# Reciprocal standard deviations computed on VectorE alone in a four-layer network on one core

## The chip, the cores and the metric

The kernel runs on one core of a Trainium2 chip. The metric is device time in microseconds (us) of one execution. The time before is the median of three runs. The profile is that of one more execution, with a time of its own.

## The reference

The input x has shape 2 x 64 x 64 x 128 and float32 values. Four layers follow each other, and each adds its result to x:

- layer 0: group norm over 32 groups of channels, then four-headed attention over 4096 tokens with a relative position bias, `softmax(q k / sqrt(32) + pos) v`
- layer 1: group norm, then a triangular multiplication: layer norm, gated projections, a product over one spatial axis, a second layer norm and a projection
- layer 2: layer norm, attention with `silu(scores * scores)` in place of a softmax, causal, plus a positional term; self and positional part are joined and pass a layer norm over 256 channels; then a mixture of 64 experts
- layer 3: layer norm, softmax attention; then a mixture of 8 experts

What the change touches is one expression, which every norm contains:

```python
v = jnp.var(x, axis=axis, keepdims=True)
return (x - m) / jnp.sqrt(v + eps)
```

The kernel takes means and variances on VectorE and needs `1/sqrt(var + eps)` for tiles of 128 partitions by n numbers, with n = 1, 4, 8, 24 or 32.

## The kernel before, in words

**The helper.** `rstd_parts` (L97 to L112) makes the reciprocal deviations of one tile. It adds eps on VectorE (L101, tile rs_v), takes the square root on ScalarE (L105, rs_s), the reciprocal on VectorE (L108, rs_r), and one Newton step on VectorE: q = -0.5 r r (L110), q = q v (L111), out = (q + 1.5) r (L112). It is a generator: where the caller asks for `apart`, it yields after L101; it always yields after the square root. Callers that schedule by hand run what stands between two yields as one piece. `rstd` (L92) runs all pieces at once.

**Who calls it.** 52 calls are executed:

- Layer 0 calls it through `tokens` (L438, n = 1) for each of two images: the first ahead of the attention loop, the second as pieces inside it. While the first runs, GpSimd builds the table `ka` (L301, 16 products of 32x1024) and VectorE waits on no one else. The result `gr` goes into the normalisation L447, that into the key projection L482, and from there by transfers into the first scores (L800).
- Layer 1 calls it through `group_scale` (L146, n = 1) twice, and through `ln_stats` (L158, n = 8) for 8 groups of the first norm (L1092) and 8 of the second (L1151, tiles named l1o). The compiler's scheduler orders these instructions; GpSimd multiplies at L1089, L1161 and L1183.
- Layer 2's attention calls it through `norm_stats` (L1325, n = 4, 4, 24 and 32) and through `join` (L1471, n = 4), once for each of 16 blocks of 512 queries.
- Layer 2's experts call `ln_stats` 8 times with n = 8 (L1726); layer 3's attention and experts call it for each image with n = 32 (L171 and around).

A fallback branch of layer 0 (around L904) holds calls too; it isn't executed.

**Layer 2's attention.** It is ordered by hand. One step k of a query block issues, in this order: eight score matmuls in two pairs (L1527; the PSUM tile `sc` has two buffers), the square of the first pair on ScalarE (L1541), the scaling of the second pair on VectorE (L1551) and its square on GpSimd (L1554), two silus on ScalarE of the two steps before (L1565), and the matmuls with the values of three steps before (L1579). After this a planner (`some`, L1302 to L1308) runs pieces of the work that is due: by the number of pieces left over the number of steps left it takes so many pieces from `chain` (keys, statistics, joins, outputs) and from `fill` (the positional matmuls L1428). The pieces of a join are: transposes and a copy (L1457); the statistics L1462 and L1463 and four products L1465; then rs_v with the square root; then reciprocal and Newton step. After it come the pieces of the output (L1480 to L1502). An instruction of a piece stands in its engine's queue behind what the step has issued, and ahead of all that the next step issues.

Of the kernel before, what the change touches and what calls it, by code (L numbers as in the profile page):

```python
# [8 lines left out]
F32 = mybir.dt.float32  # L9
AF = mybir.ActivationFunctionType  # L10
ALU = mybir.AluOpType
# [3 lines left out]
P = 128  # L15
# [23 lines left out]
class Net:  # L39
# [57 lines left out]
    def rstd_parts(self, out, var, eps, n, apart=False):  # L97

        nc = self.nc
        v = self.small.tile([P, n], F32, tag=f"rs_v{n}", name="rs_v", bufs=4 if n < 8 else 2)  # L100
        nc.vector.tensor_scalar(v, var, eps, None, ALU.add)  # L101
        if apart:
            yield
        s = self.small.tile([P, n], F32, tag=f"rs_s{n}", name="rs_s", bufs=4 if n < 8 else 2)
        nc.scalar.activation(s, v, AF.Sqrt)  # L105
        yield
        r = self.small.tile([P, n], F32, tag=f"rs_r{n}", name="rs_r", bufs=4 if n < 8 else 2)
        nc.vector.reciprocal(r, s)  # L108
        q = self.small.tile([P, n], F32, tag=f"rs_q{n}", name="rs_q", bufs=4 if n < 8 else 2)
        nc.vector.scalar_tensor_tensor(q, r, -0.5, r, ALU.mult, ALU.mult)  # L110
        nc.vector.tensor_tensor(q, q, v, ALU.mult)  # L111
        nc.vector.scalar_tensor_tensor(out, q, 1.5, r, ALU.add, ALU.mult)  # L112

    def group_stats(self, ps, b, xT=None):

# [2103 lines left out]
```

## Time and profile before

| What | Value |
|---|---|
| time before, median of three runs | 4488.38 us (4481.65 to 4494.05) |
| the profiled execution's own time | 4491.71 us |
| its span | 4489.8 us |
| PE (TensorE) busy | 4093.3 us, 91% |
| DVE (VectorE) busy | 2932.6 us, 65% |
| ACT (ScalarE) busy | 2488.6 us, 55% |
| POOL (GpSimd) busy | 912.0 us, 20% |
| activation table loads by L105 | 25, 1283 ns each |
| activation table loads in all | 52 |

The share of an engine is an average over four very different layers, so a share says little about one place. In timeline lines the columns are start and duration in us, the engine, the line, the operation, the tiles (out<-in), the sizes and the count; brackets give the idle time ahead of it and what ended it. An activation table load (ACT_TABLE_LOAD) is a ScalarE instruction which the compiler puts ahead of an activation of another family of functions; it is named by the line of that activation. PEld is TensorE's loading of weights.

### The profile page before, as it was taken

What the parts mean: (1) busy time and instruction counts of PE and PEld (TensorE: products, weight loads), DVE (VectorE), ACT (ScalarE), POOL (GpSimd) and SP (SyncE); (2) the same over time, 40 slices, a digit from 0 to 9 for tenths busy, and PEclk for the clock granted to TensorE, in tenths of its full rate; (3) what the DMA queues carried; (4) which work ended last, traced back from release to release, by engine and by line L of the source; (5) the groups of instructions that cost most, each with busy time, mean ns of one, the idle gap of its engine ahead of it and who ended that gap; (6) DMA issues with size and microseconds to landing.
All of it is one profiled execution on the core that took longest, in us unless ns stands there. A gap on an engine that the chain in (4) does not pass through costs nothing.

```text
span 4489.8 us, 66995 instructions
## 1 busy us (share of the span) xinstructions
PE 4093.3 (91%) x26440; PEld 1633.4 (36%) x26440; DVE 2932.6 (65%) x4641; ACT 2488.6 (55%) x3267; POOL 912.0 (20%) x667
## 2 busy tenths in 40 slices
PE   6999999999999948468999899998689999999979
PEld 3233333333333326322233223332364444444453
DVE  4888888998999979745566656656253333333358
ACT  3777777777777724235777688785123222322225
POOL 4110011020000030113455455552000000000015
PEclk7999999999999968678999999997889999999969
DMA  6453335454333300000000000002610000000001
GB/s 174 93 135 62 69 84 137 76 123 89 59 60 61 61 9 1 10 18 1 1 1 1 1 1 1 1 1 88 177 40 0 0 0 1 0 0 1 0 10 34
DMA packets 200764, 189.10 MB, mean 42 GB/s; under 512 B 83546, under 2 KB 137658, under 8 KB 200250
## 3 DMA queue, kind: packets, MB, share of 16 engines
q1 hardware_dynamic: 196986, 179.35, 18.1%
q10 hardware_dynamic: 3072, 4.34, 0.4%
q8 instruction: 210, 3.44, 0.3%
q0 software_dynamic: 384, 1.05, 0.1%
q14 instruction: 112, 0.92, 0.1%
HBM read 143.78 MB, written 45.09 MB: 42 GB/s over the span
## 4 chain that ended last, share of the span: by engine, by line
PE 47%; DVE 9%; ACT 4%; issue 1%; SPq 1%; DMA 1%; POOL 0%; DVEq 0%; ACTq 0%; POOLq 0%
PE oTl L1954 10%; PE scl L1937 10%; PE l2sc L1527 5%; PE l2pos L1428 5%; PE l2av L1579 5%; PE f3ex L2121 2%; ACT l2es L1565 2%; SPq L1682 1%; PE l2pu L1412 1%; DVE l2es L1551 1%; DVE l1t L1117 1%; ACT l2es L1541 1%; PE l2po L1486 1%; PE l3pq L1889 1%; PE prl L1976 1%
## 5 line engine op out<-in xcount | busy, mean ns | idle before, releaser
L813 DVE TENSOR_TENSOR l0acc<-l0acc,l0es 128x1024 f32<-128x1024 f32 x960 | 1230.6, 1282 | 133.1 <-ACT l0es L808 39.3
L808 ACT ACTIVATE l0es<-l0sc 128x1024 f32<-128x1024 f32 x1024 | 952.4, 1053 | 284.7 <-PE l0sc L800 267.8
L800 PE MATMUL l0sc<-l0mv,ka 64*64 64x512 f32 x8192 | 921.7, 596 | 21.1 <-DMA l0mv<-l0hd 16.3
L1962 DVE TENSOR_TENSOR accl<-accl,esl 128x1024 f32<-128x1024 f32 x240 | 294.0, 1225 | 520.1 <-ACT esl L1948 482.1
L1554 POOL TENSOR_TENSOR l2es<-l2es 128x1024 f32<-128x1024 f32 (+3 forms) x288 | 505.0, 1753 | 603.9 <-DVE l2es L1551 532.8
L1948 ACT ACTIVATE esl<-scl 128x1024 f32<-128x1024 f32 x240 | 245.5, 1023 | 547.0 <-PE scl L1937 547.0
L1565 ACT ACTIVATE l2es<-l2es 128x1024 f32<-128x1024 f32 (+3 forms) x576 | 533.3, 977 | 6.9 <-POOL l2es L1558 6.7
L800 PEld LDWEIGHTS l0sc<-l0mv,ka 64*64 64x64 f32 x8192 | 294.5, 132 | 640.9 <-ACT l0es L808 296.8
L1551 DVE TENSOR_SCALAR l2es<-l2sc 128x1024 f32<-128x1024 f32 (+3 forms) x272 | 306.4, 1126 | 297.2 <-PE l2sc L1527 294.5
L1937 PE MATMUL scl<-l3qT,l3kT 128*128 128x512 f32 x1024 | 482.4, 593 | 0.9 <-DVE l3v L1903 0.9
L831 PE MATMUL l0o<-l0es,l0v 128*32 128x512 f32 x4096 | 465.6, 595 | 0.0
L1954 PE MATMUL oTl<-esl,l3v 128*128 128x512 f32 x960 | 448.5, 592 | 0.0
L1541 ACT ACTIVATE l2es<-l2sc 128x1024 f32<-128x1024 f32 (+3 forms) x288 | 273.4, 949 | 261.3 <-PE l2sc L1527 258.2
L1527 PE MATMUL l2sc<-l2q,l2kT 32*128 32x512 f32 (+3 forms) x2304 | 340.5, 625 | 10.0 <-DVE l2es L1551 5.8
L1579 PE MATMUL l2av<-l2es,l2v 128*32 128x512 f32 (+3 forms) x2304 | 321.6, 579 | 8.8 <-ACT l2es L1565 8.7
L1428 PE MATMUL l2pos<-l2v,toe 128*32 128x512 f32 (+3 forms) x2304 | 299.5, 581 | 1.4 <-ACT l2v L1373 1.4
L745 POOL TENSOR_TENSOR l0os<-l0os,l0rr 128x512 f32<-128x512 f32 x32 | 63.2, 1975 | 1152.0 <-ACT l0rr L742 1091.3
L2133 POOL TENSOR_TENSOR f3part<-f3part 128x256 f32<-128x256 f32 x64 | 46.5, 726 | 1204.3 <-ACT f3part L2130 1204.3
L1937 PEld LDWEIGHTS scl<-l3qT,l3kT 128*128 128x128 f32 x1024 | 192.2, 190 | 231.1 <-issue 226.5
L1954 PEld LDWEIGHTS oTl<-esl,l3v 128*128 128x128 f32 x960 | 182.4, 190 | 229.6 <-issue 225.5
L831 PEld LDWEIGHTS l0o<-l0es,l0v 128*32 128x32 f32 x4096 | 121.4, 109 | 304.1 <-issue 299.5
L1527 PEld LDWEIGHTS l2sc<-l2q,l2kT 32*128 32x128 f32 x2304 | 100.9, 189 | 255.0 <-ACT l2es L1565 91.7
(468 smaller groups left out, 3915.6 us busy)
## 6 DMA issues: line engine op xcount, KB each, us to landing
l0mv<-l0hd SPq DMA_DIRECT2D x254, 128.0 KB
l0mv<-l0qd SPq DMA_DIRECT2D x124, 256.0 KB
f2w<-in_L_ffn_weight_dram SPq DMA_DIRECT2D x16, 1024.0 KB
f2w<-in_L_ffn_weight_dram SPq DMA_DIRECT2D x64, 256.0 KB
l0mv<-l0wd SPq DMA_DIRECT2D x126, 128.0 KB
l0sh<-l0eh SPq DMA_DIRECT2D x60, 144.0 KB
l0tw<-l0sw SPq DMA_DIRECT2D x64, 128.0 KB
l0wd<-l0rw SPq DMA_DIRECT2D x16, 512.0 KB
```

Of the source, the lines that this page charges most:

```text
L800: nc.tensor.matmul(sc[64 * c : 64 * c + 64, h, :], lhsT=ka[rows, k0 : k0 + 64], rhs=mv[rows, NX - 1 - yb, :], start=True, stop=True,)
L808: nc.scalar.activation(es[yb, s], sc, AF.Exp)
L813: nc.vector.tensor_tensor(cur.acc, cur.acc, es[yb, s], ALU.add)
L831: nc.tensor.matmul(cur.o[lo : lo + HD, :], lhsT=v[:, 2 * (xb * NX + yb) + s, HD * h : HD * (h + 1)], rhs=es[yb, s][:, h, :], start=(xb == ...
L1428: nc.tensor.matmul(pos[c : c + 32, j0:, :], lhsT=toe[:, d * P + c : d * P + c + 32], rhs=v[:, n0 + j0 - d : n0 + 4 - d, :], start=(d == n0 ...
L1527: nc.tensor.matmul(sc[:, h2, off:], lhsT=kT[hs, cols], rhs=q[hs, off:], start=True, stop=True,)
L1551: nc.vector.tensor_scalar(es[:, :, lo:], sc[:, :, lo:], root, None, ALU.mult)
L1554: nc.gpsimd.tensor_tensor(part, part, part, ALU.mult)
L1565: nc.scalar.activation(e[:, :, off:], e[:, :, off:], AF.Silu)
L1579: nc.tensor.matmul(avs[i][hs, off:], lhsT=vs[b][:, k, hs], rhs=es[h // 2][:, h % 2, off:], start=(k == 0), stop=last,)
L1937: nc.tensor.matmul(sc[:, i, :], lhsT=kT[:, k * P : (k + 1) * P], rhs=qs, start=True, stop=True,)
L1954: nc.tensor.matmul(oT, lhsT=v[:, k, :], rhs=es[:, i, :], start=(k == 0), stop=(k == NC - 1),)
```

## The change

The square root on ScalarE and the reciprocal go. A first value of the reciprocal root is made from the bits of v, read as an integer: bits times -0.5 plus 0x5F3759DF, read as a float again. Three Newton steps follow in place of one. The fixed yield stands after the first Newton step now; the yield of `apart` stays where it was.

```diff
         nc.vector.tensor_scalar(v, var, eps, None, ALU.add)
         if apart:
             yield
-        s = self.small.tile([P, n], F32, tag=f"rs_s{n}", name="rs_s", bufs=4 if n < 8 else 2)
-        nc.scalar.activation(s, v, AF.Sqrt)
-        yield
         r = self.small.tile([P, n], F32, tag=f"rs_r{n}", name="rs_r", bufs=4 if n < 8 else 2)
-        nc.vector.reciprocal(r, s)
+        nc.vector.tensor_scalar(
+            r.bitcast(mybir.dt.int32),
+            v.bitcast(mybir.dt.int32),
+            -0.5,
+            float(0x5F3759DF),
+            ALU.mult,
+            ALU.add,
+        )
         q = self.small.tile([P, n], F32, tag=f"rs_q{n}", name="rs_q", bufs=4 if n < 8 else 2)
-        nc.vector.scalar_tensor_tensor(q, r, -0.5, r, ALU.mult, ALU.mult)
-        nc.vector.tensor_tensor(q, q, v, ALU.mult)
-        nc.vector.scalar_tensor_tensor(out, q, 1.5, r, ALU.add, ALU.mult)
+        for i in range(3):
+            nc.vector.scalar_tensor_tensor(q, r, -0.5, r, ALU.mult, ALU.mult)
+            nc.vector.tensor_tensor(q, q, v, ALU.mult)
+            nc.vector.scalar_tensor_tensor(out if i == 2 else r, q, 1.5, r, ALU.add, ALU.mult)
+            if i == 0:
+                yield
```

In the built order of instructions, PE, POOL and SP keep theirs. ACT loses 52 square roots, and its table loads fall from 52 to 6. DVE has six instructions more in each call, 312 in all that are executed: eleven instead of five. In layer 1 and in layer 2's experts they stand between the statistics of the next group; in the parts ordered by hand they stand together, as the pieces say.

## The prediction

> **What bounds the kernel now.** I read the page first, then all instructions of the square root's line, then timelines where it stands. The page says that TensorE is the wide bound, with VectorE second:
>
> ```profile
> PE 4093.3 (91%) x26440; PEld 1633.4 (36%) x26440; DVE 2932.6 (65%) x4641; ACT 2488.6 (55%) x3267; POOL 912.0 (20%) x667
> ```
>
> The line of the square root, with shortest, median and longest in ns:
>
> ```profile
> L105 ACT ACTIVATE rs_s<-rs_v x52: 203/208/229, 18.7 to 4306.0; 128x8 f32<-128x8 f32 x24, 128x4 f32<-128x4 f32 x18, 128x32 f32<-128x32 f32 x5, 128x1 f32<-128x1 f32 x4
> L105 ACT ACT_TABLE_LOAD  x25: 1283/1283/1283, 12.5 to 4304.7; - x25
> ```
>
> The reader sees what can be won at most: 52 roots of 0.208 us, and 46 of 52 loads (25 here, the others where the previous function is loaded back) of 1.283 us, 69.8 us of ScalarE, an engine 45% idle. What counts is the place. The first call is in layer 0, before any attention:
>
> ```profile
> 10.20 19.86 POOL L301 TENSOR_TENSOR ka<-l0rev 32x1024 f32<-32x1024 f32 x10
> ...
> 18.54 0.16 DVE L101 TENSOR_SCALAR rs_v<-gpv 128x1 f32<-128x1 f32 x1 [0.74 <-PE gpv L436]
> ...
> 18.97 0.16 DVE L108 RECIPROCAL rs_r<-rs_s 128x1 f32<-128x1 f32 x1 [0.27 <-ACT rs_s L105]
> 19.16 0.61 DVE L110 SCALAR_TENSOR_TENSOR rs_q<-rs_r 128x1 f32<-128x1 f32 x1
> ...
> 19.81 1.85 DVE L111 TENSOR_TENSOR rs_q<-rs_q,rs_v 128x1 f32<-128x1 f32 x1
> ...
> 21.69 1.85 DVE L112 SCALAR_TENSOR_TENSOR gr<-rs_q,rs_r 128x1 f32<-128x1 f32 x1
> ```
>
> One number per partition takes 0.16 us with one SBUF operand and 1.85 us with two, while GpSimd multiplies (1.99 us each, 16 until 34.7): every such step waits for one GpSimd product. Elsewhere L110 takes 0.17 at the median and 1.87 at most. Laid over GpSimd's products, 29 of 52 L110 lie free (mean 0.16 us) and 23 overlap (mean 1.23), while the reciprocal is at 0.20 either way.
>
> The second place is a join of layer 2's attention, 16 in all. Its chain of waits, then its timeline:
>
> ```profile
> 2171.69 1.28 ACT L105
> 2172.97 0.01 issue
> 2172.98 0.20 ACT rs_s L105
> 2173.18 0.91 ACT l2es L1541
> 2174.10 0.02 issue
> 2174.11 1.28 ACT L1565
> ```
>
> ```profile
> 2174.61 1.89 POOL L1554 TENSOR_TENSOR l2es<-l2es 128x1024 f32<-128x1024 f32 x1 [0.63 <-DVE rs_r L108]
> 2174.65 1.87 DVE L110 SCALAR_TENSOR_TENSOR rs_q<-rs_r 128x4 f32<-128x4 f32 x1
> ...
> 2176.84 1.22 DVE L1551 TENSOR_SCALAR l2es<-l2sc 128x1024 f32<-128x1024 f32 x1
> ...
> 2177.47 1.05 PE L1579 MATMUL l2av<-l2es,l2v 128*32 128x512 f32 x4 [0.37 <-ACT l2es L1565]
> ```
>
> Both loads lie on the chain. But in the same step VectorE's L110 waits for GpSimd's square, and L1551, which frees a score buffer, stands behind it. The third place is layer 1, from the windows:
>
> ```profile
> core 0: us, PE busy (x) PEld busy (x) DVE busy (x) ACT busy (x) POOL busy (x), PEclk, DMA share, GB/s
> 1640.00:1720.00 80.00, 34.10 (x128) 23.91 (x127) 64.42 (x219) 17.96 (x35) 24.71 (x15) 0.59 0.00 1
> ...
> 1935.00:3095.00 1160.00, 1073.57 (x7801) 342.76 (x7800) 680.44 (x1129) 854.10 (x966) 568.35 (x368) 0.96 0.00 1
> ```
>
> In layer 1's norm VectorE is busy 64 of 80 us and TensorE 34: what VectorE gets more of is paid there, and ScalarE's loads cost nothing. In layer 2's attention TensorE leads with 1074 of 1160.
>
> **Part by part.** A call loses a root (0.21) and a reciprocal (0.16 to 0.20), and gets the seed and six two-operand steps more. No row shows a product on integers; L101 has the same shape (0.16), and I take it, so the seed pays for the reciprocal. Were its conversion as dear as another whole instruction, it would be 52 x 0.16 = 8 us at most; nothing suggests that it costs less than L101. Dependent small steps start 0.20 us apart (1653.53, .73, .93 in layer 1); six are 1.2 us where nothing else fills the gaps, and 0.08 to 0.17 each between other instructions.
>
> *Start of layer 0.* Three waits for a product become nine: six more of 1.88 us (start to start) are 11.3. Without ScalarE's round trip (18.73 to 18.97) the seed starts at once, -0.2. VectorE is then done at 34.8, just as GpSimd ends, and the first normalisation L447 takes 0.8 us, as it does alone, not 2.4: -1.6. Sum +9.5 (7 to 11.5). Projections, transfers and the first score at 87.3 follow in series, TensorE standing idle for 14.5 us before that score, so nothing hides it.
>
> *Second call in layer 0.* Inside a loop where TensorE is busy 1483 of 1500 us; at its two loads (429.96 and 434.30) it idles 0.77. I take -0.5.
>
> *Layer 1.* First norm: 8 groups x 0.8 (between 0.5 filled and 1.2 dependent; more with GpSimd's 24.7 of 80 us, which stalled L110 for 1.65 in one group) and two group norms x 0.9: +8 (4 to 13). Second norm: VectorE sets a period of some 8.7 us, 8 x 0.7 = +5.5 (3 to 11). Nothing is gained: ScalarE is busy 18 of 80.
>
> *Layer 2's statistics.* n = 24 at the start, TensorE waiting for them: 1.2 less the round trip 0.4, +0.8. n = 32 in the loop: two loads go, taken like a join's below, -1.5.
>
> *Joins.* Gone: 2.77 us of ScalarE in two neighbouring steps. These took 4.34 and 5.06 us against 2.93 to 3.06 of others; the first was late because VectorE was still at the join's L1465. TensorE's values waited from 2176.04 to 2177.47: 1.4 us, which I take as the gain. Added: the seed and three steps in one piece, six in the next. The first piece now meets the square of 2172.09 (before, only L101 stood there): VectorE reaches L1551 1.0 to 1.4 us later. The second piece, about 2.8 us with one wait, lets the next L1551 start 1.7 us later than before. VectorE has 1.1 us of slack in a step, and TensorE needs the buffer: 0.4 + 0.75 lost. Net -0.25 each, **-4** for 16. If the delays hide, -1.4 x 16 = -22; if both are paid in full, +1.25 x 16 = +20.
>
> A rule of the Trainium skill speaks against the change here (SBUF — State Buffer, "Who interferes with whom"): a VectorE instruction with two SBUF inputs and a GpSimd instruction that reads SBUF exclude each other for a whole instruction, in order of issue. Read alone, it lets each of six added steps wait for a square of 1.89: 11.3 us a join, +181 in all. The row says how often: one L110 of 1.87 and then L111 and L112 of 0.16 each, because GpSimd does one square a step, which starts only after L1551. So a piece meets one, and I take one more wait a join. On the other side the Trainium skill (ScalarE: Activation LUTs, "What ACT_TABLE_LOAD costs") puts a switch at 1.28 us plus a drain of 1.38, which would make 46 of them 122 us; here a load ends at 2175.39 and silu starts at 2175.41, so it is 59 us.
>
> *Layer 2's experts*, 8 calls, VectorE busy 80% of a period, six steps of 0.08 to 0.2 each: 0.4 a call, +3 (0 to 6). *Layer 3's norms*: 1.2 less the longer part of the round trips, +0.7; *its experts' second norm*, where the reciprocal waited 2.61 us for ScalarE at 4306.23 and TensorE idled 1.19: -1.2.
>
> Sum: 9.5 - 0.5 + 8 + 5.5 + 0.8 - 1.5 - 4 + 3 + 0.7 - 1.2 = **+20.3**. The profiled execution would take 4491.7 + 20.3 = 4512.0 (span 4489.8 and 1.9 around it); it lay 3.3 above the median of the runs, so the forecast is 4488.4 + 20.3 = **4508.7**.
>
> **The rivals.**
>
> *The other side, faster: loads on ScalarE's chain.* Near the end of the image ScalarE itself runs from piece to piece in the chain, and a join's pieces show 1.28 + 0.20 + 1.28 = 2.76 us in it. If that is what a join is worth and VectorE's delays hide, 16 x 2.76 = -44 in place of -4, so 4508.7 - 40 = 4468.5. It wins over the rest from a price of 1.5 us a join (24.3 / 16), and shows as faster from 2.4. Against it: part of these loads lay where TensorE still had work, and VectorE is the next in line in just these steps.
>
> *Within 0.3%: layer 1 hides it.* The gaps of the scheduled parts take the added steps, and layer 2's experts too: 13.5 + 3 becomes 5: 4508.7 - 11.5 = 4497. For it: interleaved instructions start 0.08 us apart. Against it: the steps depend on each other.
>
> *Slower still: joins bound by VectorE.* Both delays paid, +20 in place of -4: 4533.
>
> *That the change doesn't do what it says* is excluded: six loads are left in the built order.
>
> **The numbers.** Some 0.3% (13.5 us) is what a measurement of this kernel can tell, so "same" is 4475 to 4502. The forecast has a chance of 0.5, joins bound by VectorE 0.2, hidden in layer 1 0.2, faster 0.1. The forecast's own range, 4496 to 4522, reaches a little below 4502, so slower gets 0.67, same 0.25, faster 0.08. The range goes from 4486, where joins gain half of what the rival says, to 4533.
>
> **What would show it.** L110 to L112 of the first call at 1.85 us nine times, L447's first at 0.8 and the first score near 97; layer 1 some 13 us longer; no load in joins, the values no longer late, but L1551 late behind rs_q and score matmuls waiting for it. I am wrong if joins get over 1 us shorter, or if GpSimd's products no longer hold up VectorE at the start.

## The result and the profile after

The changed kernel takes 4512.97 us (median of five runs, 4511.44 to 4518.77), against 4488.0 before (now the median of five runs): a ratio of 1.0057, 95% interval 1.0046 to 1.0069. That is 25.0 us slower; the forecast was 4508.7, 20.3 slower.

The profiled execution is the slowest of the five; its span is 4516.7 us, 26.9 above that of before. First the busy line of its page:

```profile
PE 4094.2 (91%) x26440; PEld 1644.2 (36%) x26440; DVE 3000.4 (66%) x4953; ACT 2422.7 (54%) x3169; POOL 910.6 (20%) x667
```

ScalarE lost 66 us of the 70 counted beforehand. VectorE has 312 instructions and 68 us more. At the 0.16 us of a free small instruction 312 would be 50, and the 52 seeds stand for the 52 reciprocals: by this estimate some 18 us more of VectorE's busy time is waiting. The timeline of the first call in layer 0 (VectorE alone) shows the waits (rows left out are marked "...", here and below):

```profile
18.74 0.15 DVE L105 TENSOR_SCALAR rs_r<-rs_v 128x1 int32<-128x1 int32 x1
18.93 0.86 DVE L115 SCALAR_TENSOR_TENSOR rs_q<-rs_r 128x1 f32<-128x1 f32 x1
19.82 1.85 DVE L116 TENSOR_TENSOR rs_q<-rs_q,rs_v 128x1 f32<-128x1 f32 x1
...
25.46 0.16 DVE L116 TENSOR_TENSOR rs_q<-rs_q,rs_v 128x1 f32<-128x1 f32 x1
25.66 1.77 DVE L117 SCALAR_TENSOR_TENSOR rs_r<-rs_q,rs_r 128x1 f32<-128x1 f32 x1
...
33.12 0.81 DVE L454 TENSOR_SCALAR l0mv<-l0xT,gm,gr 128x1024 f32<-128x1024 f32 x1
```

Seven of nine two-operand steps take 1.77 to 1.85 us, one 0.86, and one slips through at 0.16. The normalisation starts at 33.12 in place of 23.57, and is quick (0.81), GpSimd being nearly done. The join that the prediction looked at, 22 us later, with GpSimd's squares (POOL):

```profile
2194.35 1.90 POOL L1561 TENSOR_TENSOR l2es<-l2es 128x1024 f32<-128x1024 f32 x1 [2.93 <-DVE rs_v L101]
2194.38 1.89 DVE L105 TENSOR_SCALAR rs_r<-rs_v 128x4 int32<-128x4 int32 x1
...
2196.70 0.16 DVE L117 SCALAR_TENSOR_TENSOR rs_r<-rs_q,rs_r 128x4 f32<-128x4 f32 x1
2196.78 1.22 DVE L1558 TENSOR_SCALAR l2es<-l2sc 128x1024 f32<-128x1024 f32 x1
...
2198.05 0.30 PEld L1534 LDWEIGHTS l2sc<-l2q,l2kT 32*128 32x128 f32 x4 [0.52 <-DVE l2es L1558]
2198.08 1.89 POOL L1561 TENSOR_TENSOR l2es<-l2es 128x1024 f32<-128x1024 f32 x1 [1.84 <-DVE rs_q L115]
2198.11 1.89 DVE L116 TENSOR_TENSOR rs_q<-rs_q,rs_v 128x4 f32<-128x4 f32 x1
```

Each piece waits once for GpSimd, 1.89 us. In the first piece it is the seed that waits, an instruction with one tensor operand. The chain of waits at this join no longer holds ScalarE, but VectorE's L1558 and then TensorE:

```profile
2193.14 1.14 DVE l2es L1558
...
2194.32 1.13 PE l2sc L1534 x4
...
2197.30 1.88 PE l2sc L1534 x8
```

A step of before that nothing holds up has this row in its chain:

```profile
2180.10 1.07 PE l2sc L1527 x8
```

That is the price: eight score matmuls take 1.88 us instead of 1.07, because the second pair waits for L1558 (the PEld row at 2198.05), which stood behind the seed.

TensorE has the same 26440 matmuls in the same order in all kernels of this study (in candidates a and b two in layer 2's experts change places). So a stage can be measured between the same two matmuls in each trace. The table is worked out in that way, in us. Its first column runs from TensorE's first matmul; layer 1 is two stretches, of before about 1607 to 1722 and 1810 to 1893; a join is measured from the start of the third step behind its transposes to that of the sixth:

| Kernel traced | start, to the first projection | layer 1, both norms | join, three steps, mean of 15 |
|---|---|---|---|
| before | 20.97 | 199.2 | 12.25 |
| after | 28.97 | 217.1 | 12.36 |
| root in joins | 28.94 | 215.0 | 12.24 |
| scalar operands at the start | 17.28 | 215.5 | 12.36 |
| two Newton steps | 24.76 | 208.9 | 12.11 |
| root but in some places | 21.01 | 199.4 | 12.39 |
| joins in PSUM | 28.93 | 217.2 | 11.29 |
| layer 1 in PSUM | 28.74 | 192.8 | 12.36 |
| candidate a | 17.18 | 193.1 | 11.29 |
| candidate b | 17.48 | 194.9 | 11.39 |
| candidate c | 17.25 | 194.5 | 12.19 |
| two-step candidate | 17.25 | 193.3 | 11.25 |

Of the 26.9 us between the spans, 8.0 lie at the start, 18.0 in layer 1, and 1.7 in joins (15 x 0.11). The experts of layer 3 give back 1.4. What is left, some +0.6 net, is a sum of larger differences of both signs. The largest is a stage of layer 2's attention, from 2000 to 2120, which took 7.3 us less after than before. Other kernels show 115 and 120 us there with the root in the joins, and 113 to 120 without. The stage between the same matmuls, by windows of before and after, with TensorE's granted clock in the column PEclk:

```profile
core 0: us, PE busy (x), PEclk, DMA share, GB/s
2000.00:2120.00 120.00, 103.37 (x614) 0.87 0.00 1
```

```profile
2030.00:2142.00 112.00, 95.46 (x610) 0.94 0.00 1
```

The clock is 0.87 in one and 0.94 in the other, TensorE is busy for 168 and 156 ns a matmul, and no call of the helper stands there. Layer 0's loop took 4.7 more, 1518 before and 1523 after, and scatters up to 1528 over the traces. Its first stretch, from 110 to 420, lies ahead of the second call, and its code is that of before: it takes 310 us before, 312 after, and up to 318 in other traces.

### The profile page after: what moved, and what is told of

Its sections match the earlier page's. It is cut to its first block, busy times and chain, and to the rows that moved or that the text cites. A ratio compares the mean times of both kernels' runs of the same rounds, so it can differ in the third digit from the quotient of the medians.

```text
span 4516.7 us, 67206 instructions
## 1 busy us (share of the span) xinstructions
PE 4094.2 (91%) x26440; PEld 1644.2 (36%) x26440; DVE 3000.4 (66%) x4953; ACT 2422.7 (54%) x3169; POOL 910.6 (20%) x667
## 4 chain that ended last, share of the span: by engine, by line
PE 47%; DVE 12%; issue 2%; ACT 1%; DMA 1%; SPq 1%; POOL 0%; DVEq 0%; ACTq 0%; POOLq 0%
PE oTl L1961 10%; PE scl L1944 10%; PE l2sc L1534 6%; PE l2pos L1435 5%; PE l2av L1586 4%; PE f3ex L2128 2%; DVE l2es L1558 2%; PE l2pu L1419 1%; SPq L1689 1%; DVE l1t L1124 1%; PE l2po L1493 1%; DMA f2w<-in_L_ffn_weight_dram 1%; PE l3pq L1896 1%; PE f3pl L2062 1%; PE prl L1983 1%
## 5 line engine op out<-in xcount | busy, mean ns | idle before, releaser
L1558 DVE TENSOR_SCALAR l2es<-l2sc 128x1024 f32<-128x1024 f32 (+3 forms) x272 | 306.5, 1127 | 272.5 <-PE l2sc L1534 272.2
L1534 PE MATMUL l2sc<-l2q,l2kT 32*128 32x512 f32 (+3 forms) x2304 | 353.8, 615 | 14.4 <-DVE l2es L1558 6.2
L1586 PE MATMUL l2av<-l2es,l2v 128*32 128x512 f32 (+3 forms) x2304 | 306.6, 573 | 0.8 <-ACT l2es L1572 0.8
```

Source lines behind the costliest of these rows:

```text
L1534: nc.tensor.matmul(sc[:, h2, off:], lhsT=kT[hs, cols], rhs=q[hs, off:], start=True, stop=True,)
L1558: nc.vector.tensor_scalar(es[:, :, lo:], sc[:, :, lo:], root, None, ALU.mult)
L1586: nc.tensor.matmul(avs[i][hs, off:], lhsT=vs[b][:, k, hs], rhs=es[h // 2][:, h % 2, off:], start=(k == 0), stop=last,)
```

## The experiments

Every ratio is to the kernel before, run beside the experiment; the interval is the 95% one. The forecasts start from the changed kernel's 4513. The diffs show the decisive lines alone.

**Root kept in the joins.** The changed kernel, with a parameter:

```diff
-                yield from self.rstd_parts(rs[i], mv[:, :, 1], 1e-3, 4)
+                yield from self.rstd_parts(rs[i], mv[:, :, 1], 1e-3, 4, how="sqrt")
```

> The changed kernel, with the square root on ScalarE and one Newton step kept in the 16 joins alone. Theory: a join is nearly a wash, because the seed and the added steps put a second wait for GpSimd's square ahead of L1551's scaling and so give back what the two table loads cost; the two traces laid over each other put a join at -0.3 us. Undone in the joins: 4513 + 16 x 0.3 = 4518 us (4513 to 4521). Rival: the loads are worth what the chain shows, 2.76 us each: 4513 + 44 = 4557. Other rival: joins are bound by VectorE and cost 1.25 each now: 4493.

Measured: 4519.72 (4512.36 to 4525.85), ratio 1.0073 (1.0060 to 1.0086). Both rivals, 4557 and 4493, are out. The size is read from the table: 12.24 against 12.36, so undoing it in the joins gains 0.12 us each, 2 in all. The median stands above that of the changed kernel all the same, and their intervals overlap: that it came out near the 4518 of the expectation is luck. The -0.3 of the expectation was the join that I had looked at (13.04 to 12.72, as did six others by 0.3 to 0.5); six got 0.1 to 0.2 longer, and those at 2296 and 2706 got 1.6 longer. Beside these two, TensorE multiplies the values of short diagonal steps (128x384, 128x256 and 128x128 in place of 128x512), so it has less to do and the late L1558 can show in full; that this is the reason was not tested.

**Scalar operands at the start.** Only in the first call:

```diff
-            nc.vector.scalar_tensor_tensor(q, r, -0.5, r, ALU.mult, ALU.mult)
-            nc.vector.tensor_tensor(q, q, v, ALU.mult)
-            nc.vector.scalar_tensor_tensor(out if i == 2 else r, q, 1.5, r, ALU.add, ALU.mult)
+            nc.vector.tensor_scalar(q, r, r, -0.5, ALU.mult, ALU.mult)
+            nc.vector.tensor_scalar(q, q, v, 1.5, ALU.mult, ALU.add)
+            nc.vector.tensor_scalar(out if i == 2 else r, r, q, None, ALU.mult)
```

> The changed kernel, but in the first call of layer 0 (n = 1) each Newton step is written with one tensor operand and its other factors as per-partition scalars; as many instructions, in the same order. Theory: the start loses 7.7 us because two-operand instructions wait for GpSimd's products; with one operand each takes 0.16 us, the result is there near 20.9 in place of 33.1, the first normalisation is slow again (2.4 in place of 0.8), and the first projection comes some 10.5 us earlier: 4513 - 10.5 = 4502.5. Rival: the number of dependent steps costs it, whatever their operands are: 4513. Should the scalar operands wait for GpSimd too, it is 4513 as well, and the trace shows durations of 1.85.

Measured: 4505.51 (4497.09 to 4516.16), ratio 1.0044 (1.0031 to 1.0057). VectorE's timeline of the same nine steps, the first and last, and GpSimd's products beside them:

```profile
18.92 0.21 DVE L148 TENSOR_SCALAR rs_q<-rs_r 128x1 f32<-128x1 f32 x1
...
20.91 0.21 DVE L150 TENSOR_SCALAR gr<-rs_r,rs_q 128x1 f32<-128x1 f32 x1
21.16 3.35 DVE L495 TENSOR_SCALAR l0mv<-l0xT,gm,gr 128x1024 f32<-128x1024 f32 x2
```

```profile
17.83 8.46 POOL L347 TENSOR_TENSOR ka<-l0rev 32x1024 f32<-32x1024 f32 x4
```

As many instructions, as dependent as before, and GpSimd is multiplying beside them: none waits. The first projection comes 11.7 us earlier than after, and 3.7 earlier than before; the medians lie 7.5 apart, and their intervals just meet, so the stage shows it more clearly than the whole. It was the second tensor operand, not the count.

**Two Newton steps.** In every call:

```diff
-        for i in range(3):
+        for i in range(2):
```

> The changed kernel with two Newton steps in place of three in every call, three VectorE instructions fewer a call. Theory: the loss is paid by the added steps: at the start 3 waits of 1.88 go and the normalisation gets slower by 1.6 (-4), layer 1 gets back half of its 18 us (-9), layer 2's experts -1.5, a join -0.3 (-5): 4513 - 19 = 4494. Rival: the loss belongs to the call as such, to the seed's integer form and to the root that no longer overlaps: 4511.

Measured: 4493.57 (4488.15 to 4512.36), ratio 1.0014 (1.0007 to 1.0020), as the theory of the steps has it. Against the changed kernel, the start is 4.2 us shorter, layer 1 8.2 and a join 0.25. This run takes away instructions and waits together; the runs with PSUM below part them.

**The change only where it should gain.** Seed and three steps in joins, layer 0's second call, the second image's statistics and layer 3; elsewhere `how="sqrt"`.

> The seed and three steps only in joins, in layer 0's second call, in the statistics of layer 2's second image and in layer 3; the square root of before at the start, in layer 1, in layer 2's first statistics and in its experts. Theory: only places that gain are left: joins -5, second call -1.2, statistics -1.5, layer 3 -2.3, so 4488 - 10 = 4478 (4472 to 4484). Rival, that the differences seen in layer 2's attention are TensorE's clock and not the change: 4488.

Measured: 4488.10 (4485.67 to 4497.82), ratio 1.0000 (0.9992 to 1.0008). The theory of this run falls. The 5 us put down to the joins were the -0.3 of one join, taken 16 times: the table has the joins at 12.39 in the mean, 0.14 worse than before and so +2 in all, while layer 3's experts give back 1.4. The number of the rival came true; its reason, TensorE's clock, holds for the stage from 2000 to 2120, which takes 120 us here as before.

**Joins without waits.** The step is regrouped so that each instruction has one operand in SBUF and one in PSUM, the memory that TensorE writes its products to; v and e lie in columns of the join's own bank, read out by then:

```diff
-            nc.vector.scalar_tensor_tensor(q, r, -0.5, r, ALU.mult, ALU.mult)
-            nc.vector.tensor_tensor(q, q, v, ALU.mult)
-            nc.vector.scalar_tensor_tensor(out if i == 2 else r, q, 1.5, r, ALU.add, ALU.mult)
+            nc.vector.tensor_tensor(e, v, r, ALU.mult)
+            nc.vector.scalar_tensor_tensor(e, e, -0.5, r, ALU.mult, ALU.mult)
+            nc.vector.scalar_tensor_tensor(out if i == 2 else r, e, 1.5, r, ALU.add, ALU.mult)
```

> The changed kernel, but in the joins the Newton steps are regrouped as e = v r, e = -0.5 e r, r = (e + 1.5) r with v and e in PSUM, in columns of a bank that the join has already used: as many instructions, each with one SBUF operand. Theory: a join gains nothing because two waits for GpSimd's squares (1.9 us each) stand ahead of L1551's scaling. Without them the values no longer wait for the table loads and nothing is late in their place: some 1.3 us a join, 4513 - 20 = 4493 (4486 to 4500). Rival: the plain length of eleven small instructions makes L1551 late, waits or not: 4511.

Measured: 4499.03 (4493.02 to 4505.34), ratio 1.0023 (1.0014 to 1.0032). VectorE's timeline at the same join, and GpSimd's square beside it:

```profile
2204.17 0.16 DVE L127 TENSOR_SCALAR rs_r<-l2st 128x4 int32<-128x4 int32 x1
2204.36 0.17 DVE L140 TENSOR_TENSOR l2st<-l2st,rs_r 128x4 f32<-128x4 f32 x1
...
2205.36 1.23 DVE L1600 TENSOR_SCALAR l2es<-l2sc 128x1024 f32<-128x1024 f32 x1 [0.43 <-PE l2sc L1576]
```

```profile
2204.14 1.89 POOL L1603 TENSOR_TENSOR l2es<-l2es 128x1024 f32<-128x1024 f32 x1 [2.93 <-DVE l2st L106]
```

The square runs from 2204.14 to 2206.03, and seed and steps pass beside it at 0.16 to 0.17 each, and none of the helper's 176 rows in the 16 joins takes more than 0.18; the scaling now waits for TensorE (0.43), not TensorE for it. A join takes 11.29, so 1.07 less than after (16 us in 15 joins) and 0.96 less than before. The plain length of eleven small instructions is nearly hidden.

**Layer 1 without waits.** The same regrouping in layer 1's 16 layer norms, with a PSUM tile of their own.

> The changed kernel, with the regrouped steps (v and e in PSUM) in layer 1's 16 layer norms alone. Theory: of the 18 us that layer 1 got longer, six plain instructions a call explain about 12 (16 x 6 x 0.12), and waits for GpSimd the rest; in PSUM the waits of the steps that were there before go too, as far as they don't move to the next instruction: 4513 - 12 = 4501. Rival: only the number of instructions counts, since VectorE does them one after the other and GpSimd's work must be done anyway: 4513.

Measured: 4495.46 (4481.12 to 4505.77), ratio 1.0014 (1.0006 to 1.0023). Layer 1's norms take 192.8 us: 24.3 less than after, twice what I expected, and 6.4 less than before. A norm in the trace of after shows the waits, with GpSimd's product above the seed:

```profile
1660.56 2.35 POOL L1096 TENSOR_TENSOR l1y<-l1y,l1gb 128x1024 f32<-128x1024 f32 x1 [5.76 <-DVE mv_l L163]
1660.75 2.19 DVE L105 TENSOR_SCALAR rs_r<-rs_v 128x8 int32<-128x8 int32 x1
...
1662.97 1.18 DVE L115 SCALAR_TENSOR_TENSOR rs_q<-rs_r 128x8 f32<-128x8 f32 x1
1664.19 1.18 DVE L116 TENSOR_TENSOR rs_q<-rs_q,rs_v 128x8 f32<-128x8 f32 x1
```

Three waits in a row, the seed's the longest. The corresponding norm with v and e in PSUM:

```profile
1654.39 2.34 POOL L1144 TENSOR_TENSOR l1y<-l1y,l1gb 128x1024 f32<-128x1024 f32 x1 [4.45 <-DVE mv_l L204]
1654.58 0.17 DVE L127 TENSOR_SCALAR rs_r<-rs_l 128x8 int32<-128x8 int32 x1
1654.78 0.17 DVE L140 TENSOR_TENSOR rs_l<-rs_l,rs_r 128x8 f32<-128x8 f32 x1
```

Counted over the helper's rows of these 16 calls, what exceeds 0.175 us a row is 28.7 us before, 35.4 after and 0.0 here. So most of what this run takes away is waiting that was there before the change; the change added 6.7 us of waiting and, in 96 more rows, some 14 us of plain instructions.

**Candidates.** The first kernel, candidate a, puts together what the experiments showed to gain: scalar operands in layer 0 and the group norms, the root with one regrouped step in layer 1's layer norms, seed and three regrouped steps in the joins, the root of before in layer 2's first statistics and experts. Candidate b has the seed in layer 1 too; candidate c the root with one regrouped step in the joins; the last is a with two steps in joins, second statistics and layer 3.

```diff
-                yield from self.rstd_parts(rs[i], mv[:, :, 1], 1e-3, 4)
+                at = [pt[:, 0, 4 * k : 4 * k + 4] for k in range(2)]
+                yield from self.rstd_parts(rs[i], mv[:, :, 1], 1e-3, 4, at=at)
```

> A candidate to beat both: scalar-operand steps in layer 0 and in the group norms; ScalarE's root and one regrouped step with v and e in PSUM in layer 1's layer norms; seed and three regrouped steps in PSUM in the joins; the kernel of before in layer 2's first statistics and experts. Theory of the waits: start -4, layer 1 -8, joins -18, layer 3 -2 against before: 4488 - 32 = 4456 (4450 to 4470). Rival, that only the number of instructions counts: start and layer 3 alone, 4483.

> The same candidate, but with the seed and three regrouped steps in PSUM in layer 1 too: six VectorE instructions more a call than the other candidate, and no root. Theory: the plain price of the six, 0.1 each between other instructions, 16 x 0.6 = 10 us above it: 4466. Rival, that the waits were all that cost: equal to it.

> The first candidate with ScalarE's root in the joins too, and one regrouped step with v and e in PSUM: the two table loads are back in each join, six VectorE instructions a join are gone, and nothing waits for GpSimd in either. It prices the loads by themselves. Theory: a join's loads hold up the values by 1.4 us, as the trace of before showed at one join, so 4460 + 16 x 1.4 - 16 x 0.2 = 4479. Rival: without the waits ScalarE's loads hide beside the rest: 4460.

> The first candidate with two Newton steps in place of three in the joins, in the second image's statistics and in layer 3. Theory: without waits for GpSimd, three instructions more of 0.17 to 0.2 in a step with 1.1 us of slack cost a join 0.2 at most: 4460 - 3 = 4457, not to be told from the candidate. Rival: VectorE bounds the joins' steps, and each instruction counts in full: 4460 - 16 x 0.5 = 4452.

| Candidate | median us | lowest to highest | ratio to before (95%) |
|---|---|---|---|
| a | 4459.98 | 4449.55 to 4474.29 | 0.9932 (0.9917 to 0.9947) |
| b | 4464.37 | 4454.78 to 4469.85 | 0.9940 (0.9926 to 0.9955) |
| c | 4470.78 | 4468.32 to 4472.89 | 0.9960 (0.9947 to 0.9974) |
| two steps | 4457.22 | 4450.50 to 4465.89 | 0.9931 (0.9917 to 0.9945) |

All four beat both kernels. Candidate a stands 4 us off its forecast; the table's stages say where it gains: start 3.8, layer 1 6.1, joins 14.4 (15 x 0.96). Candidate b costs 1.8 us in layer 1's norms, not 10: six instructions more a call that wait for nothing are nearly paid for by the root's round trip that goes, and by the gaps between others. The plain instructions of the change are cheap there because nothing waits any more. Candidate c prices the loads where nothing waits for GpSimd: a join of 12.19 against 11.29, 0.90 us net of six small instructions, less than the 1.4 of the expectation and not zero. At the join that the 1.4 was read from it is 1.37 (13.01 against 11.64). Two steps in place of three are not told from a by the runs (0.04 a join).

## Why the prediction was right, point by point

- **The sum, +20.3; measured +25.0, and +26.9 between the spans.** The direction is as told, and so are the start and layer 1; the joins are not. The terms that the traces can price sum to some +27; layer 0's loop outside its second call (+5.8) and the stage from 2000 to 2120 (-7.3), where no line of the change runs, nearly cancel. That is luck, and each of them is larger than the forecast's miss of 4.7.
- **Start, +9.5; measured +8.0.** The mechanism is as told; the second experiment takes it away. Eight of nine steps waited and not all nine in full, since one fell between two products. The first score came at 95.0 in place of 87.3, so nothing hid it.
- **Layer 1, +8 and +5.5; measured +12.0 and +5.9.** This term was mis-sized. The prediction read a wait of 1.65 "in one group"; in before L110 takes 1.64 to 1.71 in four of the first norm's eight groups, and 0.54 to 0.58 in two. VectorE was held up there already, by 28.7 us in the helper's rows; some 14 us of added instructions and 6.7 us more waiting made the two norms 18 us longer. Where nothing waits, the same step from root to seed costs 1.8 us (candidate b against a) and not 18.
- **Seed "pays for the reciprocal": wrong where GpSimd is at work.** In before the reciprocal took 0.19 beside GpSimd and 0.21 alone, and I gave the seed the price of L101. With n = 1 it is right (0.15, in the one call beside GpSimd). Of 18 seeds with n = 4, 15 overlap a GpSimd product: 11 of these take 1.89 and four 0.17. With n = 8, six of layer 1's 16 take 1.15 to 2.33. With v in PSUM the same instruction takes 0.16 beside the square. The section of the Trainium skill that I cited (SBUF — State Buffer, "Who interferes with whom") has a sentence for it that I had left out: `tensor_scalar` can run in a mode that uses both port pairs, and then it and GpSimd exclude each other with one operand too. The runs show the wait, not the mode. Rows of before hinted at it: L101 with n = 8 took 1.81 at the median in layer 1's second norm, where GpSimd ran.
- **Joins, -4; measured +1.7: the sign was wrong.** The forecast of -0.25 was right for the join that it was read from (13.04 to 12.72) and wrong for the mean of 15 (+0.11). In the mean the loads are worth 0.90 us and not 1.4; the two waits of the changed join cost 1.07, against the forecast's 1.15 for what is added. That 1.15 is not what its working gives: delays of 1.0 to 1.4 and 1.7 less a slack of 1.1 each are 0.6 to 0.9, and in full they outweigh the gain by 1.3 to 1.7, not by 1.25. The bound from both sides (-22 to +20) held it, and the rule's reading by rows did too: one wait a piece, not one a step. In the first piece it was the seed that waited, which the prediction had not foreseen.
- **Faster by the loads on ScalarE's chain (the rival): excluded.** Its 2.76 us a join would need 44 us; candidate c shows 0.90 where nothing waits for GpSimd. The chain of waits named ScalarE, and shortening it by 2.76 moved the end by a third.
- **Joins bound by VectorE (the rival), +1.25 each: excluded** as a mean; two joins lost 1.6.
- **Layer 0's second call, -0.5; measured -1.1:** between the same matmuls around its loads (428 to 440) 11.8 us before, 10.7 in each of the other eleven traces.
- **Layer 2's experts, +3; measured +1.5** between 3110 and 3160; what follows them scatters by more than 10 us over the traces (122 to 136). **Layer 3's experts, -1.2; measured -1.4.** **Layer 3's norms, +0.7:** no cost is seen (3300 to 3345 is 0.3 shorter, 3800 to 3860 equal).
- **First statistics of layer 2, +0.8:** TensorE got them 1.6 later, but kernels with the same code there differ by 1.9, so this stays open. **Statistics of n = 32, -1.5:** not seen; from 2120 to 2150 it is 30.0 us before and 30.1 after.

## What to carry to other kernels

Before moving a small computation to VectorE, look at what GpSimd does in that moment: here an instruction of 0.16 us cost up to a whole GpSimd instruction when it needed two operands from SBUF, and in some places when it needed one. Rewriting it so that one operand lies in PSUM, or is a per-partition scalar, cost no instruction and took the waits away here, at the start, in layer 1 and in the joins. A load on the chain of waits is worth what is left when the next engine's work is counted, 0.90 of 2.76 us here. And one join is not the mean: price a place that recurs over all its copies.

## What the runs showed that was not expected

A seed with one SBUF operand can wait for GpSimd with four or eight columns (1.89 and 2.19 us in the rows above); with one column it did not (0.15 in the one call beside GpSimd, and 0.21 in the nine scalar-operand steps). TensorE's granted clock differs from trace to trace in the same stage (0.87 and 0.94 in the windows above, and 0.88 with the root kept in the joins), which goes with 7 us in a stage of 120: more than most single terms of this prediction, so that stages of two traces have to be compared with the clock beside them.
